# The end of a recommendation kernel in another order: what stands ahead of the head's results

## The chip, the cores and the metric

The kernel runs on one core of a Trainium2 chip. The metric is the device time of one execution in microseconds (us), lower is better; the time before is the median of three runs. The profile is of one execution, taken by the hardware profiler. Engines are named as the profile names them: PE (TensorE matmul) and PEld (its weight loads), DVE (VectorE), ACT (ScalarE), POOL (GpSimd), SP (SyncE, which here only starts DMAs). L142 is line 142 of the kernel.

## The reference

A batch of 16,384 users, each with a history of 200 items, an item and a category; embeddings have 64 numbers, the attention unit 36 hidden numbers.

```python
def dice(x, alpha, axis):
    mean = jnp.mean(x, axis=axis, keepdims=True)
    var = jnp.var(x, axis=axis, keepdims=True)
    p = jax.nn.sigmoid((x - mean) * jax.lax.rsqrt(var + EPS))
    return x * (p + alpha * (1.0 - p))
u = u_emb[user]          # 16384 x 64
it = i_emb[item]
c = c_emb[cate]
h = i_emb[hist]          # 200 x 16384 x 64
itb = jnp.broadcast_to(it[None], h.shape)
feat = jnp.concatenate([h, itb, h - itb, h * itb], axis=-1)
a = dice(feat @ au_W1 + au_b1, au_alpha, axis=1)
w = a @ au_W2 + au_b2
cur = jnp.sum(w * jax.lax.stop_gradient(h), axis=0)
z = jnp.concatenate([u, it, c, cur], axis=-1)
z = dice(z @ W1 + b1, alpha1, axis=0)
z = dice(z @ W2 + b2, alpha2, axis=0)
return z @ W3 + b3
```

Each history position has its own mean and variance over the whole batch, and so has each layer of the head. That is why a chunk of rows can't be finished in one go: the statistics over all eight chunks come first.

## The kernel before, in words

**Chunks and steps.** The batch is cut into ND = 8 chunks of 2,048 rows. A history position is eight steps, one for each chunk, so K = 200 x 8 = 1600 steps `step(k)`. In step k POOL gathers the embedding rows of chunk k (`fetch`, L118: one gather brings 128 rows, so 16 or 15 per step); some rows are brought instead by single DMAs on the queues of SP and ACT. One step later the chunk is transposed (`turn`, L137) and multiplied (`product`, L142); three steps later its hidden values `xs` are added up and measured (L387, L392); LAG = 10 steps later it is weighed:

- `gate(k)`: ACT writes the sigmoid of `xs` to `pg` (L362).
- `weights(k)`: DVE makes one weight per row from it (L366, L367, L368, L369, L372), which end up in `pg`.
- `weigh(k)`: DVE multiplies the history rows by their weights (L382, the last reader of `pg`) and adds the product to the running sum `cur[c]` (L384).

**The head's first layer**, one chunk at a time, is where the change is. `head_fetch(c)` has POOL gather the users' rows into `spare[c % 4]` (16 gathers, L118), and SP loads the transposed category rows `cT[c % 4]` and item rows `itT`. `head_known(c)` transposes the finished sum `cur[c]` into `hT` (DVE, L137, four instructions) and has PE multiply category, item and sum. `head_users(c)` transposes the users into `uT` (L137; for the last chunk in two parts, 12 columns of rows and then 4) and has PE multiply them. Both use `head_layer`, which writes two results in PSUM: `pz[1]` (32 rows, by the weights `w1b`) and `pz[0]` (128 rows, by `w1a`). A chunk's eight pairs of weights and data make 16 matmuls, each two instructions on PE. Then ACT adds the biases and writes `zb` (L616) and `za` (L619, into the `xs` buffer of the same chunk), and DVE takes their statistics (`measure_head`, L595; `zb` once per four chunks).

**What sets the order.** The code is written out by hand (`manual_schedule`): each engine gets its instructions in the order of the calls and works them off in that order; semaphores make it wait for data and for free buffers. The end, from L625 on, calls for j = 0 to 7 the loads of chunk j, then one or two steps, then `head_known` and `head_users` for the chunks whose sum is finished. After it come the statistics of the first layer over all chunks (`head_moments`), the second and third layer, and the output.

In the profile's names, `rows` are history or user rows, `itp` stands for `cT` and `uT` (they share storage), `px` for `pz[0]` and `pz[1]`, `xs` for `za`, and `rows` also for `zb`, which lies in a buffer of rows.

Of the kernel before, what the change touches and what calls it, by code (L numbers as in the profile page):

```python
# [10 lines left out]
AF = mybir.ActivationFunctionType  # L11
# [10 lines left out]
LAG = 10  # L22
XR = 8
TURNED = 2
ITEMS = 4
# [14 lines left out]
def din_kernel(  # L40
# [93 lines left out]
    def transpose(dst, of, n0=0, n1=TD):  # L134
        for i in range(2):
            for e in range(2):
                nc.vector.transpose(by_tile(dst[ts(e, D)], i)[:, n0:n1], of[ts(i, D), n0:n1, ts(e, S)])  # L137
# [222 lines left out]
    def gate(k, between):  # L360
        i = k // ND % 3
        nc.scalar.activation(pg, xs[k % XR], AF.Sigmoid, bias=shifts[i], scale=rstds[i])  # L362
        between()
# [34 lines left out]
    def load_items(k):  # L398
        nc.sync.dma_start(itT[k % ITEMS], items[k % ND])
# [31 lines left out]
    def step(k):  # L431

        def has(j):
            return 0 <= j < K

        def some(n):
            by_scalar.pump(min(by_scalar.done + n, by_scalar.until(k + 1)))

        if has(k + 2):
            load_items(k + 2)  # L440
        if has(k):
            l, c = divmod(k, ND)
            if c == 0 and l + 2 < L:
                load_hist_ids((l + 2) % IDX, l + 2)
            if c == 0 and l + 2 == L:
                load_ids(ids[1], r_user)
            if c == 1 and l + 2 < L:
                load_list(l + 2)
            fetch(k)
            q, m = side(k) or (None, None)  # L450
            taken = q and q.take(m)
        by_sync.pump(by_sync.until(k + 1))
        norm = has(k - 3) and (k - 3) % ND == ND - 1
        if has(k - LAG) and not norm:
            gate(k - LAG, lambda: some(5))
        if has(k):
            place(k, taken)
        if has(k - 1):
            turn(k - 1)
        if has(k - 3):  # L460
            hidden(k - 3)
            measure(k - 3)
        if norm:
            moments((k - 3) // ND)
            some(20)
            if has(k - LAG):
                gate(k - LAG, lambda: some(5))
        by_scalar.pump(by_scalar.until(k + 1))
        if has(k - 1):
            product(k - 1)  # L470
        if has(k - LAG):
            weights(k - LAG)
            weigh(k - LAG)
        if has(k) and k % ND == ND - 2 and k // ND + 2 < L:
            scale_list(k // ND + 2)
# [117 lines left out]
    def measure_head(i, j, t):  # L593
        for h in range(2):
            nc.vector.bn_stats(zst[i][:, 2 * j + h, :], t[:, ts(h, CH)])  # L595

    def head_fetch(c):
        for n in range(TD):
            i = c * TD + n
            gather(spare[c % 4], ids[1][:, i : i + 1], n, u_emb)  # L600
# [3 lines left out]
    def head_layer(pairs, first, last):  # L604
        layer(pz[1][:S], [(w1b[:, f], t) for f, t in pairs], first=first, last=last)
        layer(pz[0], [(w1a[:, f], t) for f, t in pairs], first=first, last=last)

    def head_known(c):
        transpose(hT[c % TURNED], cur[c].rearrange("p (n d) -> p n d", d=D))
        head_layer(((2, cT[c % 4]), (1, itT[(K + c) % ITEMS]), (3, hT[c % TURNED])), True, False)  # L610

    def head_users(c):
        for n0, n1 in ((0, LATE), (LATE, TD)) if c == ND - 1 else ((0, TD),):
            transpose(uT[c % 4], spare[c % 4], n0, n1)
        head_layer(((0, uT[c % 4]),), False, True)
        nc.scalar.activation(zb[c // 4][ts(c % 4, S)], pz[1][:S], AF.Identity, bias=b1b)  # L616
        if c % 4 == 3:
            measure_head(1, c // 4, zb[c // 4])
        nc.scalar.activation(za[c], pz[0], AF.Identity, bias=b1a)  # L619
        measure_head(0, c, za[c])  # L620

    with tc.manual_schedule():
        for k in range(K):
            step(k)
        k, c = K, 0  # L625
        for j in range(ND):
            head_fetch(j)
            nc.sync.dma_start(cT[j % 4], cates[j])
            load_items(K + j)
            while k <= K + (j + 1) * LAG // ND:  # L630
                step(k)
                k += 1
            while c <= j and k > K + LAG - ND + c:
                head_known(c)
                head_users(c)
                c += 1
        assert k > K + LAG - 1 and c == ND

        def head_moments(parts):

            n = len(parts)
            mv = small.tile([P, n, 2], F32, tag=f"hmv{n}", name="hmv")
            for j, (i, _) in enumerate(parts):
                nc.vector.bn_aggr(mv[:, j], zst[i].rearrange("p c s -> p (c s)"))
            for j, (_, same) in enumerate(parts):
                nc.tensor.matmul(pg[:, j : j + 1], same, mv[:, j, 0:1], start=True, stop=True)
            mean = small.tile([P, n], F32, tag=f"hmean{n}", name="hmean")
            nc.vector.tensor_copy(mean, pg[:, :n])
            dev = small.tile([P, n], F32, tag=f"hdev{n}", name="hdev")
            nc.vector.tensor_sub(dev, mv[:, :, 0], mean)  # L650
            nc.vector.tensor_mul(dev, dev, dev)
            nc.vector.tensor_add(dev, dev, mv[:, :, 1])
            for j, (_, same) in enumerate(parts):
                nc.tensor.matmul(py[:, j : j + 1], same, dev[:, j : j + 1], start=True, stop=True)
            rstd = small.tile([P, n], F32, tag=f"hrstd{n}", name="hrstd")
            root(rstd, py[:, :n])
            shift = small.tile([P, n], F32, tag=f"hshift{n}", name="hshift")
            nc.vector.scalar_tensor_tensor(shift, mean, -1.0, rstd, ALU.mult, ALU.mult)
            return [(rstd[:, j : j + 1], shift[:, j : j + 1]) for j in range(n)]

        temps = [hm, *flat_rows[6:8]]
        turns = iter(range(1000))

        def dice(dst, z, norm, al1, al):
            p = temps[next(turns) % len(temps)]
            nc.scalar.activation(p, z, AF.Sigmoid, bias=norm[1], scale=norm[0])
            nc.vector.tensor_scalar(p, p, al1, al, ALU.mult, ALU.add)
            nc.vector.tensor_mul(dst, p, z)

        z2 = flat_rows[8:]  # L670
        na, nb = head_moments([(0, same_a), (1, same_b)])
        ab = uT[:2]

        def second(c):
            nc.scalar.activation(z2[c], pz[c % 4], AF.Identity, bias=bias2)
            measure_head(2, c, z2[c])

        def first(c):
            dice(cur[c], za[c], na, al1a, ala)
            if c % 4 == 0:  # L680
                dice(ab[c // 4], zb[c // 4], nb, al1b, alb)

        first(0)
        for c in range(ND):
            if c + 1 < ND:
# [62 lines left out]
```

## Time and profile before

| | |
|---|---|
| median of three runs | 50,439.11 us |
| lowest and highest | 50,419.98 and 50,472.64 us |
| span of the profiled execution, first to last instruction | 31,394.9 us |
| median less span | 19,044.2 us |
| busy: POOL, DVE, PE | 23,583.2, 23,566.6 and 10,269.6 us |
| gathers from the item table on POOL | 24,828, of 944 ns each |
| the end: first transpose of a finished sum | at 31,117.71 us |
| last gather of users | at 31,233.05 us |
| last statistics of the head's first layer begin | at 31,320.92 us |

The profile gives no time of the profiled execution other than its span; what lies between the span and the runs' time is not seen in it. Times "at" count from the first instruction. In the profile's rows a group's idle time is that of its engine just before it, and the arrow names what ended the wait. The timeline has a start, a duration, the engine, the line, the operation with output and input, and in brackets the idle time before it.

### The profile page before, as it was taken

The numbers are of one execution on the slowest core, as the hardware profiler recorded it, in microseconds if no ns is written. First come the engines' busy times: TensorE is split into PE (matmuls) and PEld (weight loads), VectorE is DVE, ScalarE is ACT, GpSimd is POOL, SyncE is SP. The second block draws the span as 40 slices with busy tenths as digits, with TensorE's granted clock in tenths as the row PEclk, the third lists the DMA queues.
The fourth block names the chain that finished last, engine by engine and source line by source line (L and its number), as shares of the span: only waits on it lengthen the run. The fifth ranks groups of instructions, "written<-read, shape, count | busy, mean of one in ns | idle before, by whom it ended". The sixth has DMA issues, their size and how long they took to land.

```text
span 31394.9 us, 344371 instructions
## 1 busy us (share of the span) xinstructions
PE 10269.6 (33%) x13700; PEld 3833.8 (12%) x13700; DVE 23566.6 (75%) x35131; ACT 3842.2 (12%) x4167; POOL 23583.2 (75%) x24979
## 2 busy tenths in 40 slices
PE   5333333333333333333333333333333333333334
PEld 2111111111111111111111111111111111111111
DVE  6777777777777777777777777777777777777777
ACT  0111111111111111111111111111111111111111
POOL 7777777777777777777777777777777777777776
PEclk7666666666666666666666666666666666666666
DMA  2222222222222222222222222222222222222221
GB/s 60 56 56 56 55 56 55 56 56 56 56 55 56 56 55 56 55 56 56 55 56 56 56 56 55 56 56 55 56 55 56 56 56 55 56 56 55 56 56 47
DMA packets 1461708, 1742.53 MB, mean 56 GB/s; under 512 B 824822, under 2 KB 850678, under 8 KB 1459126
## 3 DMA queue, kind: packets, MB, share of 16 engines
q0 software_dynamic: 799104, 819.88, 14.8%
q1 hardware_dynamic: 544246, 885.58, 8.9%
q10 hardware_dynamic: 115776, 15.04, 0.3%
q14 instruction: 2475, 20.28, 0.2%
q8 instruction: 107, 1.75, 0.0%
HBM read 1709.80 MB, written 8.52 MB: 55 GB/s over the span
## 4 chain that ended last, share of the span: by engine, by line
POOL 62%; issue 23%; DMA 6%; DVE 6%; PE 1%; ACTq 1%; ACT 1%; SPq 0%; POOLq 0%; DVEq 0%
POOL rows L118 62%; DMA rows<-in_L_rec_i_emb,idx 6%; DVE hT L137 1%; PE py L525 1%; DVE py L366 1%; DVE pg L367 1%; DVE py L368 0%; DVE st L392 0%; DVE xs L387 0%; ACT pg L362 0%; ACTq L328 0%; PE px L142 0%; DVE other L413 0%; DVE t L158 0%; DVE t L157 0%
## 5 line engine op out<-in xcount | busy, mean ns | idle before, releaser
L118 POOL DMA_INDIRECT rows<-in_L_rec_i_emb,idx x24828 | 23446.7, 944 | 7606.2 <-issue 7362.7
L142 PE MATMUL px<-hT,blk_h 128*128 128x512 f32 x6400 | 5951.4, 1085 | 19937.4 <-DVE xs L387 19904.6
L137 DVE STREAM_TRANSPOSE hT<-rows 64x512 f32<-64x512 f32 x6400 | 4514.8, 705 | 6602.8 <-DMA rows<-in_L_rec_i_emb,idx 6298.5
L142 PEld LDWEIGHTS px<-hT,blk_h 128*128 128x128 f32 x6400 | 1873.7, 323 | 23103.2 <-DVE xs L387 21419.7
L142 PE MATMUL px<-hm,blk_m 128*128 128x512 f32 x6400 | 4114.5, 777 | 995.5 <-DVE hm L403 995.5
L362 ACT ACTIVATE pg<-xs,sh,rs 128x1024 f32<-128x1024 f32 x1600 | 1931.7, 1207 | 16036.0 <-issue 7328.8
L396 ACT COPY py<-hT 128x1024 f32<-128x1024 f32 x1600 | 1626.1, 1016 | 9705.2 <-DVE hT L137 9643.5
L142 PEld LDWEIGHTS px<-hm,blk_m 128*128 128x128 f32 x6400 | 1797.5, 285 | 3951.9 <-DVE hm L403 2034.6
L366 DVE SCALAR_TENSOR_TENSOR py<-pg,au_1al,xs 128x1024 f32<-128x1024 f32 x1600 | 2068.0, 1293 | 81.0 <-ACT pg L362 8.6
L392 DVE BATCH_NORM_STATS2 st<-xs 128x6 f32<-128x512 f32 x3200 | 2057.8, 685 | 54.9
L367 DVE STREAM_TRANSPOSE pg<-py 128x1024 f32<-128x1024 f32 x1600 | 2024.9, 1266 | 54.5
L368 DVE TENSOR_REDUCE py<-pg 128x32 f32<-128x1024 f32 x1600 | 1972.6, 1233 | 54.4
L382 DVE TENSOR_TENSOR py<-rows,pg 128x1024 f32<-128x1024 f32 x1592 | 1955.9, 1229 | 54.6
L387 DVE TENSOR_TENSOR xs<-px,itp 128x1024 f32<-128x1024 f32 x1600 | 1958.3, 1224 | 50.4
L403 DVE TENSOR_TENSOR hm<-py,itT 128x1024 f32<-128x1024 f32 x1600 | 1934.2, 1209 | 80.2 <-ACT py L396 79.9
L384 DVE TENSOR_TENSOR cur<-py,cur 128x1024 f32<-128x1024 f32 x1592 | 1948.6, 1224 | 55.0
L372 DVE SCALAR_TENSOR_TENSOR pg<-py,au_bias,part 32x16 f32<-32x16 f32 x6400 | 1530.2, 239 | 225.6
L369 DVE COPY part<-py 64x32 f32<-64x32 f32 x1600 | 310.6, 194 | 55.5
L358 ACT COPY rows<-act_rows 128x64 f32<-128x64 f32 x450 | 109.8, 244 | 721.9 <-issue 682.2
L358 ACT COPY rows<-sp_rows 128x64 f32<-128x64 f32 x450 | 109.9, 244 | 519.9 <-issue 403.2
L524 DVE TENSOR_SCALAR cur<-pg,rows 128x512 f32<-128x512 f32 x150 | 103.0, 743 | 92.8 <-PE pg L517 89.6
L525 PE MATMUL py<-cur,cur 128*128 128x512 f32 x300 | 156.1, 663 | 42.6 <-DVE cur L524 38.2
(159 smaller groups left out, 2075.5 us busy)
## 6 DMA issues: line engine op xcount, KB each, us to landing
sp_rows<-in_L_rec_i_emb SPq DMA_DIRECT2D x57600, 0.2 KB
act_rows<-in_L_rec_i_emb ACTq DMA_DIRECT2D x57600, 0.2 KB
itT<-items SPq DMA_DIRECT2D x1608, 512.0 KB
rows<-in_L_rec_i_emb,idx POOLq DMA_INDIRECT x24828
idx<-in_r_hist SPq DMA_DIRECT2D x200, 64.0 KB
lists<-in_r_hist SPq DMA_DIRECT2D x600, 1.0 KB
items<-itT SPq DMA_DIRECT2D x8, 512.0 KB
cates<-xs SPq DMA_DIRECT2D x8, 512.0 KB
```

The costliest lines, as they stand in the source:

```text
L118: nc.gpsimd.indirect_dma_start(out=dst[:, n, :], out_offset=None, in_=table, in_offset=bass.IndirectOffsetOnAxis(ap=ids, axis=0),)
L137: nc.vector.transpose(by_tile(dst[ts(e, D)], i)[:, n0:n1], of[ts(i, D), n0:n1, ts(e, S)])
L142: nc.tensor.matmul(dst[:, ts(i, CH)], lhsT, rhs[:, ts(i, CH)], start=(first and j == 0), stop=(last and j == len(pairs) - 1), skip_group_c ...
L362: nc.scalar.activation(pg, xs[k % XR], AF.Sigmoid, bias=shifts[i], scale=rstds[i])
L366: nc.vector.scalar_tensor_tensor(py, pg, au_1al, xs[k % XR], ALU.mult, ALU.mult)
L367: nc.vector.transpose(pg, py)
L368: nc.vector.reduce_sum(total, pg.rearrange("p (n a) -> p n a", a=S), axis=mybir.AxisListType.X)
L382: nc.vector.tensor_mul(of, rows[k % ROWS], w.unsqueeze(2).to_broadcast([P, TD, D]))
L384: nc.vector.tensor_add(cur[k % ND], py, cur[k % ND])
L387: nc.vector.tensor_add(xs[k % XR], px[k % 2], itp[k % ND])
L392: nc.vector.bn_stats(stats[l % 3][:, 2 * c + i, :], xs[k % XR][:, ts(i, CH)])
L403: nc.vector.tensor_mul(hm, py, itT[k % ITEMS])
```

## The change

The calls of the end are put in another order; nothing is added or left out. `head_known` now holds only the products with category and item, a new `head_sums` the transpose of the sum and its products, and a new `head_measure` the statistics. `head_load` bundles the three loads of a chunk and is called three chunks ahead of `head_sums`. For each chunk: weights and weighted sum, the sigmoid of the chunk after it, the loads, the statistics of the chunk before, the sum's products, the users' products and ACT's two results, and then the next chunk's products with category and item.

```diff
     def head_known(c):
+        head_layer(((2, cT[c % 4]), (1, itT[(K + c) % ITEMS])), True, False)
+
+    def head_sums(c):
         transpose(hT[c % TURNED], cur[c].rearrange("p (n d) -> p n d", d=D))
-        head_layer(((2, cT[c % 4]), (1, itT[(K + c) % ITEMS]), (3, hT[c % TURNED])), True, False)
+        head_layer(((3, hT[c % TURNED]),), False, False)
...
         nc.scalar.activation(zb[c // 4][ts(c % 4, S)], pz[1][:S], AF.Identity, bias=b1b)
+        nc.scalar.activation(za[c], pz[0], AF.Identity, bias=b1a)
+
+    def head_measure(c):
         if c % 4 == 3:
             measure_head(1, c // 4, zb[c // 4])
-        nc.scalar.activation(za[c], pz[0], AF.Identity, bias=b1a)
         measure_head(0, c, za[c])
...
-        k, c = K, 0
-        for j in range(ND):
-            head_fetch(j)
-            nc.sync.dma_start(cT[j % 4], cates[j])
-            load_items(K + j)
-            while k <= K + (j + 1) * LAG // ND:
-                step(k)
-                k += 1
-            while c <= j and k > K + LAG - ND + c:
-                head_known(c)
-                head_users(c)
-                c += 1
+        first_weighed = LAG - ND
+        for c in range(first_weighed + 1):
+            head_load(c)
+            step(K + c)
+        head_known(0)
+        for c in range(ND):
+            k = K - ND + c
+            if c:
+                weights(k)
+                weigh(k)
+            if c + 1 < ND:
+                gate(k + 1, lambda: None)
+            if c + first_weighed + 1 < ND:
+                head_load(c + first_weighed + 1)
+            if c:
+                head_measure(c - 1)
+            head_sums(c)
+            head_users(c)
+            if c + 1 < ND:
+                head_known(c + 1)
+        head_measure(ND - 1)
```

With the new lines, L616 and L619 become L619 and L620, and everything behind the end's loop moves down by 18 lines.

On DVE, around chunk 1 (`xs_88` and `xs_89` are `za` of chunks 0 and 1; `hT_87<-cur_117` the transposed sum of chunk 1, `itp_131<-rows_71` its users, and `xs_90` the hidden values of chunk 2, whose weights begin with L366):

```order
 L382 TENSOR_TENSOR py<-rows_79,pg 128x1024
 L384 TENSOR_TENSOR cur_117<-py,cur_117 128x1024
+L595 BN_STATS zst_3768<-xs_88 128x6 x2
 L137 STREAM_TRANSPOSE hT_87<-cur_117 64x512 x4
 L137 STREAM_TRANSPOSE itp_131<-rows_71 64x512 x4
-L595 BN_STATS zst_3768<-xs_89 128x6 x2
 L366 SCALAR_TENSOR_TENSOR py<-pg,au_1al,xs_90 128x1024
 L367 STREAM_TRANSPOSE pg<-py 128x1024
```

Chunk 1's statistics stood between its transposes and chunk 2's weights; now chunk 0's stand behind chunk 1's weighted sum, and chunk 2's weights follow the transposes at once.

On ACT, in the first chunks (`pg<-xs_89` is the sigmoid of chunk 1; `rows_74<-px_67` and `xs_88<-px_66` are the results `zb` and `za` of chunk 0):

```order
 L362 ACTIVATE pg<-xs_88,sh_146,rs_143 128x1024
-L616 ACTIVATE rows_74<-px_67,b1b 32x1024
-L619 ACTIVATE xs_88<-px_66,b1a 128x1024
 L362 ACTIVATE pg<-xs_89,sh_146,rs_143 128x1024
-L616 ACTIVATE rows_74<-px_67,b1b 32x1024
-L619 ACTIVATE xs_89<-px_66,b1a 128x1024
+L619 ACTIVATE rows_74<-px_67,b1b 32x1024
+L620 ACTIVATE xs_88<-px_66,b1a 128x1024
 L362 ACTIVATE pg<-xs_90,sh_146,rs_143 128x1024
```

The sigmoid of chunk 1 stood behind the two results of chunk 0 and now stands ahead of them; so in every later chunk.

On PE, the second half of chunk 1's products (`itp_127` category, `itT_97` item, `hT_87` sum, `itp_131` users; `px_67` by `w1b`, `px_66` by `w1a`):

```order
 L142 MATMUL px_66<-itp_127,w1a 128x512
 L142 MATMUL px_66<-itT_97,w1a 128x512
-L142 MATMUL px_66<-hT_87,w1a 128x512
 L142 MATMUL px_66<-itp_127,w1a 128x512
 L142 MATMUL px_66<-itT_97,w1a 128x512
-L142 MATMUL px_66<-hT_87,w1a 128x512
+L142 MATMUL px_67<-hT_87,w1b 32x512 x2
+L142 MATMUL px_66<-hT_87,w1a 128x512 x2
 L142 MATMUL px_67<-itp_131,w1b 32x512 x2
 L142 MATMUL px_66<-itp_131,w1a 128x512 x2
```

The sum's products stood among those with category and item and held them up until the sum was transposed; now all of the latter come first. The orders of POOL's gathers and of SP's loads are the same as before.

More of the change, by code (lines that the diff above doesn't have):

```diff
@@ L616, in head_users, with head_load @@
         nc.scalar.activation(zb[c // 4][ts(c % 4, S)], pz[1][:S], AF.Identity, bias=b1b)
+        nc.scalar.activation(za[c], pz[0], AF.Identity, bias=b1a)
+    def head_measure(c):
         if c % 4 == 3:
             measure_head(1, c // 4, zb[c // 4])
-        nc.scalar.activation(za[c], pz[0], AF.Identity, bias=b1a)
         measure_head(0, c, za[c])
+    def head_load(c):
+        head_fetch(c)
+        nc.sync.dma_start(cT[c % 4], cates[c])
+        load_items(K + c)
     with tc.manual_schedule():
@@ L624, in din_kernel @@
             step(k)
-        k, c = K, 0
-        for j in range(ND):
-            head_fetch(j)
-            nc.sync.dma_start(cT[j % 4], cates[j])
-            load_items(K + j)
-            while k <= K + (j + 1) * LAG // ND:
-                step(k)
-                k += 1
-            while c <= j and k > K + LAG - ND + c:
-                head_known(c)
-                head_users(c)
-                c += 1
-        assert k > K + LAG - 1 and c == ND
+        first_weighed = LAG - ND
[19 more added lines that the diff above has]
+        head_measure(ND - 1)
         def head_moments(parts):
```

## The prediction

> **What bounds the kernel now.** I read the page first, then the timeline of each engine over the last 400 us, the chain of waits there, and the busy time of the stages.
>
> ```profile
> span 31394.9 us, 344371 instructions
> PE 10269.6 (33%) x13700; PEld 3833.8 (12%) x13700; DVE 23566.6 (75%) x35131; ACT 3842.2 (12%) x4167; POOL 23583.2 (75%) x24979
> L118 POOL DMA_INDIRECT rows<-in_L_rec_i_emb,idx x24828 | 23446.7, 944 | 7606.2 <-issue 7362.7
> ```
>
> For over 31 ms the kernel is a line of gathers on POOL: one takes 0.944 us and the next begins some 0.30 us later, whatever the other engines do. The change touches none of that. It rewrites the end, where the gathers run out. The stages of the end (start and end, width, busy time of PE, PEld, DVE, ACT and POOL, granted TensorE clock, DMA share, GB/s):
>
> ```profile
> 31118.00:31234.00 116.00, 75.73 (x148) 21.98 (x148) 63.44 (x90) 13.38 (x12) 87.75 (x93) 0.82 0.25 63
> 31234.00:31322.00 88.00, 56.25 (x105) 15.53 (x104) 45.73 (x68) 12.17 (x11) 0.00 (x0) 0.79 0.00 1
> 31322.00:31395.00 73.00, 48.42 (x108) 17.57 (x108) 56.18 (x102) 29.97 (x26) 0.00 (x0) 0.81 0.01 2
> ```
>
> In the middle row POOL has nothing left, no DMA moves, and yet PE is busy for 56 of 88 us and DVE for 46: the two take turns. Those 88 us are what the change can reach. The last 73 us (the head's second half) keep their instructions.
>
> One chunk in that stage, first on DVE (start, duration, idle before it and what ended the idle), then on ACT, with the chain that ended last in between:
>
> ```profile
> 31278.27 2.88 DVE L137 STREAM_TRANSPOSE itp<-rows 64x512 f32<-64x512 f32 x4
> 31293.63 1.29 DVE L595 BATCH_NORM_STATS2 zst<-xs 128x6 f32<-128x512 f32 x2 [12.48 <-ACT xs L619]
> 31294.83 1.28 DVE L366 SCALAR_TENSOR_TENSOR py<-pg,au_1al,xs 128x1024 f32<-128x1024 f32 x1
> ...
> 31301.30 1.23 DVE L384 TENSOR_TENSOR cur<-py,cur 128x1024 f32<-128x1024 f32 x1
> 31302.63 2.88 DVE L137 STREAM_TRANSPOSE hT<-cur 64x512 f32<-64x512 f32 x4
> 31305.54 3.62 DVE L137 STREAM_TRANSPOSE itp<-rows 64x384 f32<-64x384 f32 x8
> 31318.99 1.29 DVE L595 BATCH_NORM_STATS2 zst<-rows 128x6 f32<-128x512 f32 x2 [9.83 <-ACT rows L616]
> 31320.92 1.29 DVE L595 BATCH_NORM_STATS2 zst<-xs 128x6 f32<-128x512 f32 x2 [0.64 <-ACT xs L619]
> ```
> ```profile
> 31304.10 15.64 PE px L142 x28
> 31319.77 1.12 ACT xs L619
> ```
> ```profile
> 31266.22 1.20 ACT L362 ACTIVATE pg<-xs,sh,rs 128x1024 f32<-128x1024 f32 x1
> ...
> 31293.49 1.20 ACT L362 ACTIVATE pg<-xs,sh,rs 128x1024 f32<-128x1024 f32 x1
> 31317.86 1.10 ACT L616 ACTIVATE rows<-px,b1b 32x1024 f32<-32x1024 f32 x1 [23.16 <-PE px L142]
> ```
>
> The two sigmoids (L362) stand 31293.49 - 31266.22 = 27.27 us apart: that is one chunk. It is a ring without overlap: sigmoid, weights and weighted sum on DVE (31294.83 to 31302.63, 7.80 us), half of the sum's transpose, 15.64 us of matmuls, 1.12 us of ACT, 1.20 us of statistics, and only then the next chunk's weights. DVE's wait of 12.48 us in every chunk, ended by L619, is the ring's mark:
>
> ```profile
> PE px L142 <- DVE hT L137: 82.6, 8, 17.4
> ...
> DVE zst L595 <- ACT xs L619: 73.3, 8, 12.5
> ```
>
> Over the eight chunks DVE waits 73.3 us for the results, and PE 82.6 us for the transposed sum.
>
> **The change part by part.** No instruction is added or removed; all keep their shapes. Four things move.
>
> *Statistics of the chunk before (L595) go behind the next chunk's weighted sum.* In DVE's row the wait for L619 then falls behind 7.80 us of work that needs no result of the head. The next sigmoid needs `pg` free (the weighting multiply, L382, is its last reader) and stands ahead of the results on ACT, so it ends long before DVE comes to it: DVE first transposes the sum (2.88 us) and the users (2.88 us). I cost both edits at nothing on the path. The cover is those 5.8 us for the sigmoid's 1.2, and the 7.8 us for the matmuls on the users and the two ACT results. If that cover went, DVE would wait for the rest.
>
> *DVE is then the steady user.* Per chunk: 7.80 + hT 2.91 (31302.63 to 31305.54) + users 2.88 + statistics 1.20 (31293.63 to 31294.83) = 14.8 us; 1.2 us more behind chunk 3, for the second group's statistics.
>
> *PE's matmuls with category and item go ahead of the sum.* Each matmul is two instructions, 32 per chunk. Their pace has two values:
>
> ```profile
> 31194.97 1.02 PE L142 MATMUL px<-itT,w1b 128*32 128x512 f32 x2
> 31198.06 1.05 PE L142 MATMUL px<-hT,w1b 128*32 128x512 f32 x2 [2.07 <-DVE hT L137]
> ...
> 31222.44 1.92 PE L142 MATMUL px<-hT,w1b 128*32 128x512 f32 x2 [9.82 <-DVE hT L137]
> 31224.14 1.91 PE L142 MATMUL px<-itp,w1b 128*32 128x512 f32 x2
> 31225.85 1.91 PE L142 MATMUL px<-itT,w1b 128*32 128x512 f32 x2
> 31227.56 1.29 PE L142 MATMUL px<-hT,w1b 128*32 128x512 f32 x2
> 31228.77 1.12 PE L142 MATMUL px<-itp,w1a 128*128 128x512 f32 x2
> ...
> 31317.75 1.98 PE L142 MATMUL px<-itp,w1a 128*128 128x512 f32 x4
> ```
> ```profile
> 31198.06 12.73 PE px L142 x28
> ```
>
> After 2.07 us of idle time PE goes on at full pace (28 instructions in 12.73 us, 0.45 each with the gaps); after 9.82 us it starts at half ((31227.56 - 31222.44) / 6 = 0.853 us each), for about 6 us. The same 28 cost 15.64 us in the last chunk. Thus before pays 2.9 us for a slow start in most chunks. Afterwards 32 x 0.45 = 14.4 us of PE work stand against 14.8 us of DVE work. PE gets 16 of the 32 (7.2 us) while DVE weighs (7.8 us), so its gaps are around a microsecond and it stays at pace. [...]
>
> *Loads (users' gathers, cT, itT) are asked for three chunks ahead.* POOL's row keeps its order, so what matters is whether a slot is late. It was not:
>
> ```profile
> 31075.99 2.86 DVE L137 STREAM_TRANSPOSE hT<-rows 64x512 f32<-64x512 f32 x4 [5.70 <-DMA rows<-in_L_rec_i_emb,idx]
> ```
> ```profile
> 31073.24 0.94 POOL L118 DMA_INDIRECT rows<-in_L_rec_i_emb,idx  x1 [0.30 <-issue]
> 31074.48 0.95 POOL L118 DMA_INDIRECT rows<-in_L_rec_u_emb,idx  x1 [0.30 <-issue]
> ...
> 31233.05 0.94 POOL L118 DMA_INDIRECT rows<-in_L_rec_u_emb,idx  x1 [0.30 <-issue]
> ```
>
> The 128 gathers of users start from 31074.48 to 31233.05, (31233.05 - 31074.48) / 127 = 1.249 us apart: 20.0 us per chunk without a stop. This becomes the new limit, since a chunk needs only 14.8 us. A gather's data can be used 31075.99 - 31073.24 = 2.75 us after its start (the last history gather and the transpose that waits for it). SP's queue is passed by two loads per chunk; each waits for a slot that was read two chunks earlier, and nothing else stands behind it.
>
> The sum, in the profiled execution's time. Chunk 0's transposes stand where they stood:
>
> ```profile
> 31117.71 2.88 DVE L137 STREAM_TRANSPOSE hT<-cur 64x512 f32<-64x512 f32 x4
> ```
>
> - Chunk c begins its users' transpose at 31120.6 + 14.8 c, with 1.2 more from c = 4: chunk 5 at 31195.8. Its users are usable at 31074.48 + 95 x 1.249 + 2.75 = 31195.9: a tie.
> - Chunk 6 would begin at 31210.6; its users come at 31074.48 + 111 x 1.249 + 2.75 = 31215.9. From here POOL leads. That transpose ends at 31218.8.
> - Chunk 7: 7.80 + 1.20 + 2.91 gives 31230.7. Its users come in two parts: twelve of sixteen columns (their transpose is about 2.2 of the 3.62 us), then the last four, usable at 31233.05 + 2.75 = 31235.8. So 31235.8 + 1.4 = 31237.2.
> - The last 8 matmul instructions begin at about half of that transpose: 31236.5 + 8 x 0.45 = 31240.1. L619's successor 1.12: 31241.2. Statistics 1.29: 31242.5.
>
> Before, the last statistics end at 31320.92 + 1.29 = 31322.2. The gain is 79.7 us; I take 79, because every step has a few hundredths of a microsecond of issue. Span 31,394.9 - 79 = 31,316 us. The profile states only the span. The runs' median is 50,439.1 us, so 19,044 us lie outside of the span; I hold them constant and carry the gain over: 50,439.1 - 79 = 50,360 us, 0.16% less. The runs shown stand from 50,419.98 to 50,472.64, so about 0.2% (101 us) is what a measurement can tell from no change. The forecast is a real gain that lies just under that line.
>
> **Unknowns and their bounds.** The mid-case of the clock: if PE started slowly in every chunk, a chunk would cost 14.4 + 2.9 = 17.3 us of PE, which then leads DVE. From 31119.2 (first half of chunk 0's transpose) 10.1 us for its last 16 instructions and 7 x 17.3 give 31250.4, 10.3 us later than above: a gain of 69. On the other side nothing goes below the gathers' end, 31235.8. What stands behind it, the transpose, matmuls, ACT and statistics, cannot be hidden, so 80 is the ceiling inside the span.
>
> **The rivals.**
>
> 1. *The 19,044 us are not a constant, but time in which everything is slower than in the profile.* Then the gain scales by 50,439.1 / 31,394.9 = 1.607: 127 us, 50,312. Nothing in the page speaks for it; the steady 944 ns of 24,828 gathers speak for a chip that runs evenly.
> 2. *The gathers alone are slower in the timed runs.* 19,044 over the 24,979 POOL instructions is 0.76 us each. A chunk of gathers would cost 16 x (1.249 + 0.76) = 32.1 us, more than the 27.27 us ring, which would then be hidden already in the kernel before: no change, 50,439. That is also the case in which the change does not do what it says. The profile can't exclude it, but shows gathers that end 88 us ahead of the ring.
> 3. *PE never reaches its full pace, and the change is slower.* Each chunk's 32 instructions then cost 32 x 0.853 + about 1 us of gaps = 28.3 us in one row on PE, more than the ring of 27.27. From 31119.2, 16 x 0.853 + 7 x 28.3 end at 31331, and with 1.12 and 1.29 us at 31333.4: 11 us later than before, 50,450. It decides once PE's 32 instructions exceed 26 us, that is 0.82 us each. Against it: 0.45 us in the row of 28 above, after a short gap; and the new order has fewer gaps.
>
> **How the numbers follow.** Forecast (69 to 80 us of gain): 0.74. Rival 1: 0.07. Rival 2: 0.10. Rival 3: 0.02. The remaining 0.07 is for medians that move by more than the runs shown, to both sides alike. The forecast's own range: 50,360 with the runs' spread (-19 and +34 around their median) is 50,340 to 50,404. The range for 8 in 10 takes in the ends of rivals 1 and 2: 50,305 to 50,440. Faster by over 0.2% means under 50,338: rival 1, a fifth of the forecast by the runs' spread, and a little of the rest, 0.24. Slower by over 0.2% needs 50,540: no mechanism here reaches it, so 0.03 from the rest. Within: 0.73.
>
> **What would show it.** In the profile after: no wait of DVE for L620 (the former L619) of more than a microsecond; L362 ahead of L619 and L620 on ACT; PE instructions 0.43 us apart through the end stage, and no start at 0.85 after chunk 1; DVE waiting for the users' gathers in chunks 6 and 7; the last user gather still at about 31233; the last L595 of `za` near 31243. The prediction is wrong if the users' gathers start later than now, if PE waits for cT or itT, or if the time outside the span moves.

## The result, and the profile after

The changed kernel takes 50,371.1 us (median of 20 runs, 50,343.0 to 50,408.4), the kernel before 50,438.4 us (20 runs, 50,420.0 to 50,472.6). The ratio is 0.9985, interval 0.9979 to 0.9992: 67 us less, where 79 were forecast. That lies inside the forecast's range and under the 0.2% named there, and the interval does not reach 1. How it came about differs from the forecast in two places, and the runs below are about these.

The page of the changed kernel: span, POOL's and DVE's share, the chain by engine, and the history's gathers.

```profile
span 50359.7 us, 344371 instructions
PE 11205.4 (22%) x13700; PEld 3875.5 (8%) x13700; DVE 23541.9 (47%) x35131; ACT 3756.0 (7%) x4167; POOL 23591.3 (47%) x24979
...
SPq 42%; issue 37%; ACTq 16%; DVE 3%; ACT 1%; PE 1%; another core or an unknown queue 0%; DMA 0%; POOL 0%; DVEq 0%; POOLq 0%
...
L118 POOL DMA_INDIRECT rows<-in_L_rec_i_emb,idx x24828 | 23454.9, 945 | 26505.3 <-DVE py L382 18667.6
```

The span is now the whole time (50,359.7 of 50,361.4 us), with the same number of instructions. So the 19 ms that stood outside the span in the first profile of before stand inside it here. POOL's gathers take 945 ns each, as before; POOL now waits 18,668 us for DVE's weighing (L382). What is slow is shown by SP's row loads of the main loop (two groups of 36 in the changed kernel, start and duration):

```profile
31070.86 38.97 SPq L328 DMA_DIRECT2D sp_rows<-in_L_rec_i_emb  x36
...
31110.38 13.77 SPq L328 DMA_DIRECT2D sp_rows<-in_L_rec_i_emb  x36
```

The same 36 instructions take 39.0 us or 13.8 us. POOL gathers until 31,093.6, beside much of the first group, and pauses beside most of the second:

```profile
31119.86 0.94 POOL L118 DMA_INDIRECT rows<-in_L_rec_i_emb,idx  x1 [26.25 <-DVE py L382]
```

The slow pace ends on SP, ACT and DVE alike at 31,099.6, 6.9 us after the last gather began (31,092.67). In the slow stretches many short instructions of SP, ACT and DVE start 0.70 or 1.40 us apart (DVE's L159, L157 and L158 at 31,094.04, 31,095.44 and 31,096.84). Long ones (1.2 us and up) hardly show it (L382's 1,592, of 1.23 us each, stood idle 57.0 us in all, 0.04 each), and not every short one does. Two of DVE's small operations in the changed kernel, four in each step (L372) and a longer row of them behind each layer (L157; behind the second bar the idle time):

```profile
L372 DVE SCALAR_TENSOR_TENSOR pg<-py,au_bias,part 32x16 f32<-32x16 f32 x6400 | 1526.9, 239 | 231.9 <-issue 5.2
L157 DVE TENSOR_TENSOR t<-rs 128x1 f32<-128x1 f32 x800 | 129.2, 161 | 931.3 <-DVE rs L159 565.4
```

That is 0.04 us of idle time an instruction against 1.16. In the first profile of before L157 had 27.7 us in all.

The end of the changed kernel by stage, in the columns of the prediction's first table: the head's first layer, a part of it, and the second half of the head.

```profile
50124.00:50286.00 162.00, 119.81 (x240) 34.40 (x240) 109.64 (x159) 25.18 (x23) 60.36 (x64) 0.86 0.12 33
50250.00:50286.00 36.00, 34.12 (x75) 9.83 (x73) 29.58 (x47) 7.75 (x7) 0.00 (x0) 1.00 0.00 0
50286.00:50360.00 74.00, 48.88 (x108) 17.68 (x108) 56.58 (x102) 29.97 (x26) 0.00 (x0) 0.80 0.01 2
```

In the middle row PE works 34 of 36 us at full clock and DVE 30: the turn-taking of before is gone. The first row holds more than that. ScalarE there (L362 sigmoid, L619 and L620 the results; in brackets the idle time before and what ended it):

```profile
50137.65 1.20 ACT L362 ACTIVATE pg<-xs,sh,rs 128x1024 f32<-128x1024 f32 x1
50161.17 1.10 ACT L619 ACTIVATE rows<-px,b1b 32x1024 f32<-32x1024 f32 x1 [22.32 <-remote]
50172.43 1.11 ACT L620 ACTIVATE xs<-px,b1a 128x1024 f32<-128x1024 f32 x1 [10.15 <-remote]
...
50222.24 1.10 ACT L619 ACTIVATE rows<-px,b1b 32x1024 f32<-32x1024 f32 x1 [32.19 <-remote]
50225.83 1.11 ACT L620 ACTIVATE xs<-px,b1a 128x1024 f32<-128x1024 f32 x1 [2.49 <-remote]
...
50252.89 1.10 ACT L619 ACTIVATE rows<-px,b1b 32x1024 f32<-32x1024 f32 x1 [10.49 <-PE px L142]
50254.86 1.11 ACT L620 ACTIVATE xs<-px,b1a 128x1024 f32<-128x1024 f32 x1 [0.87 <-PE px L142]
```

The sigmoid stands ahead of the results, as forecast. But ScalarE waits 22 and 32 us for the first results of chunks 1 and 3, where 10.5 is usual, and no recorded work ends that wait. At the second results these chunks are 21 and 23 us late. None of the four waits for a gather: in the trace the semaphores that they wait for, 128 and 127, are raised by PE and ScalarE alone. PE's last products for chunk 1 are recorded here:

```profile
50147.41 1.91 PE L142 MATMUL px<-itp,w1b 128*32 128x512 f32 x4
50149.24 1.98 PE L142 MATMUL px<-itp,w1a 128*128 128x512 f32 x4
```

They end by 50,151.2, and ACT gets the first of the two results at 50,161.17 and the second at 50,172.43. The two are 11.26 us apart, for 4 matmuls and 4 weight loads: 1.41 us an instruction, the pace of the slow stretches (1.97 us apart at 50,252.89, 3.59 in chunk 3). PE's rows, whose ends the profile models, don't show this: by them PE was done 10 us before the first of the two came. POOL at that time:

```profile
50130.94 0.94 POOL L118 DMA_INDIRECT rows<-in_L_rec_u_emb,idx  x1 [60.07 <-DVE itp L137]
...
50169.63 0.94 POOL L118 DMA_INDIRECT rows<-in_L_rec_u_emb,idx  x1 [0.30 <-issue]
50180.82 0.94 POOL L118 DMA_INDIRECT rows<-in_L_rec_u_emb,idx  x1 [10.25 <-DVE itp L137]
...
50219.51 0.94 POOL L118 DMA_INDIRECT rows<-in_L_rec_u_emb,idx  x1 [0.30 <-issue]
```

These are two bursts of 32 gathers. Chunk 1's first result comes inside the first burst, its second 2.8 us after the start of that burst's last gather, and chunk 3's first 2.7 us after that of the second (50,222.24). Whether the gathers hold the results up is the question of most runs. The same stage on DVE, changed kernel (hT is the transposition of a chunk's sum):

```profile
50124.88 2.88 DVE L137 STREAM_TRANSPOSE hT<-cur 64x512 f32<-64x512 f32 x4
...
50173.57 1.29 DVE L595 BATCH_NORM_STATS2 zst<-xs 128x6 f32<-128x512 f32 x2 [20.54 <-ACT xs L620]
...
50223.37 1.29 DVE L595 BATCH_NORM_STATS2 zst<-rows 128x6 f32<-128x512 f32 x2 [19.67 <-ACT rows L619]
...
50257.43 2.86 DVE L137 STREAM_TRANSPOSE hT<-cur 64x512 f32<-64x512 f32 x4
...
50272.06 2.86 DVE L137 STREAM_TRANSPOSE hT<-cur 64x512 f32<-64x512 f32 x4
...
50285.31 1.29 DVE L595 BATCH_NORM_STATS2 zst<-xs 128x6 f32<-128x512 f32 x2 [0.64 <-ACT xs L620]
```

Undisturbed chunks stand 14.63 us apart. In what follows "the first layer" is the time from the first hT to the end of the last L595: here 50,286.6 - 50,124.9 = 161.7 us.

### The profile page after: what moved, and what is told of

The parts are those of the page before. It is cut to its first block, busy times and chain, and to the rows that moved or that the text cites. A ratio compares the mean times of both kernels' runs of the same rounds, so it can differ in the third digit from the quotient of the medians.

```text
span 50359.7 us, 344371 instructions
## 1 busy us (share of the span) xinstructions
PE 11205.4 (22%) x13700; PEld 3875.5 (8%) x13700; DVE 23541.9 (47%) x35131; ACT 3756.0 (7%) x4167; POOL 23591.3 (47%) x24979
## 4 chain that ended last, share of the span: by engine, by line
SPq 42%; issue 37%; ACTq 16%; DVE 3%; ACT 1%; PE 1%; another core or an unknown queue 0%; DMA 0%; POOL 0%; DVEq 0%; POOLq 0%
SPq L328 35%; ACTq L328 14%; SPq L321 5%; ACTq L321 1%; SPq L399 1%; DVE py L366 1%; DVE hm L403 1%; SPq L289 1%; ACT py L396 0%; DVE pg L367 0%; DVE hT L137 0%; PE py L525 0%; DVE py L368 0%; ACT pg L362 0%
## 5 line engine op out<-in xcount | busy, mean ns | idle before, releaser
L142 PE MATMUL px<-hm,blk_m 128*128 128x512 f32 x6400 | 4915.1, 912 | 24582.9 <-DVE hm L403 24472.1
L362 ACT ACTIVATE pg<-xs,sh,rs 128x1024 f32<-128x1024 f32 x1600 | 1931.8, 1207 | 33014.7 <-issue 23975.5
L366 DVE SCALAR_TENSOR_TENSOR py<-pg,au_1al,xs 128x1024 f32<-128x1024 f32 x1600 | 2068.8, 1293 | 1112.0 <-ACT pg L362 1059.4
L382 DVE TENSOR_TENSOR py<-rows,pg 128x1024 f32<-128x1024 f32 x1592 | 1956.6, 1229 | 57.0 <-issue 2.1
L372 DVE SCALAR_TENSOR_TENSOR pg<-py,au_bias,part 32x16 f32<-32x16 f32 x6400 | 1526.9, 239 | 231.9 <-issue 5.2
L157 DVE TENSOR_TENSOR t<-rs 128x1 f32<-128x1 f32 x800 | 129.2, 161 | 931.3 <-DVE rs L159 565.4
L158 DVE SCALAR_TENSOR_TENSOR t<-t,v 128x1 f32<-128x1 f32 x808 | 130.7, 162 | 885.2 <-DVE t L157 719.1
L159 DVE SCALAR_TENSOR_TENSOR rs<-t,rs 128x1 f32<-128x1 f32 x800 | 128.3, 160 | 813.2 <-DVE t L158 678.2
```

Source lines behind the costliest of these rows:

```text
L142: nc.tensor.matmul(dst[:, ts(i, CH)], lhsT, rhs[:, ts(i, CH)], start=(first and j == 0), stop=(last and j == len(pairs) - 1), skip_group_c ...
L366: nc.vector.scalar_tensor_tensor(py, pg, au_1al, xs[k % XR], ALU.mult, ALU.mult)
L382: nc.vector.tensor_mul(of, rows[k % ROWS], w.unsqueeze(2).to_broadcast([P, TD, D]))
```

## The experiments

**e1: the kernel before, profiled once more.**

> The kernel before, unchanged, profiled once more beside the changed one. The changed kernel's profile has a span of 50,359.7 us, nearly its whole time, while the profile of before has 31,394.9: so the 19,044 us that I held constant outside of the span lie inside it in the timed runs. Theory 1 (stretches in which SP and ACT issue their single-row DMAs slowly, L328): time 50,420 to 50,473 as before, span within 3 us of it, 36 DMAs of SP's L328 in 14 to 46 us instead of 14, gathers still 0.944 us each; the end from the first transpose of a finished sum to the last statistics of the first layer takes 204 us as in the first profile, plus at most a few stretches of 30 us. Theory 2 (everything slower by 1.607): the same end takes 329 us, and one gather 1.5 us.

Measured: 50,419.8 us, and a span of 50,418.0. Its DVE:

```profile
50121.50 2.88 DVE L137 STREAM_TRANSPOSE hT<-cur 64x512 f32<-64x512 f32 x4
...
50235.35 1.29 DVE L595 BATCH_NORM_STATS2 zst<-rows 128x6 f32<-128x512 f32 x2 [27.25 <-ACT rows L616]
...
50289.81 1.28 DVE L595 BATCH_NORM_STATS2 zst<-xs 128x6 f32<-128x512 f32 x2 [12.06 <-ACT xs L619]
...
50344.08 1.29 DVE L595 BATCH_NORM_STATS2 zst<-xs 128x6 f32<-128x512 f32 x2 [0.64 <-ACT xs L619]
```

First layer 223.9 us against 204.5 in the first profile of before: the ring with its 12 us waits, and one late result (27.25 us). Like with like, the change takes 223.9 - 161.7 = 62.2 us off this stage. That is the timed gain within its interval, and the first profile was of another condition than the timed runs.

**e2 and e3: no row loads by SP and ACT, in before and after.** The edit in both:

```diff
-BY_SP = ((0, 0), (0, 3), ..., (3, 3))
-BY_ACT = ((0, 1), (0, 4), ..., (3, 4))
+BY_SP = ()
+BY_ACT = ()
```

> Kernel before with BY_SP and BY_ACT empty: no single-row DMAs on SP and ACT; POOL gathers the sixteenth row block itself. 25,872 gathers instead of 24,972. Theory 1 (the row DMAs are what is slow in the timed runs): 25,872 x 1.249 = 32,314 us plus some 280 us of end: 32,500 to 32,800 us, ratio to before 0.645 to 0.65. Theory 2 (everything is slower) or gathers alone slower (2.01 us each): 52,000 us, ratio 1.03.

> The changed kernel with BY_SP and BY_ACT empty. Theory 1: a clean end, 69 to 80 us less than e2 (79 by the sum of the prediction), its end from the first transpose of a finished sum to the last statistics 125 us against 204 in e2, PE at 0.43 us per instruction throughout, DVE waiting for the users' gathers in chunks 6 and 7. Rival (the changed kernel's own profile: 163 us for the same end, with ACT waiting 10 to 32 us ahead of its results): 163 us and about 40 us less than e2.

Measured: e2 38,329.2 us (38,327.0 to 38,338.9; ratio to before 0.7599, interval 0.7587 to 0.7612), e3 38,265.7 us (38,257.1 to 38,273.9; 0.7586, interval 0.7573 to 0.7598). I expected e2 at 32,500 to 32,800; it is slowed too, only less. For e3 I expected a clean first layer of 125 us; it took 160.4, near the rival's 163. The change is worth 63.5 us here, in the first layer 222.5 - 160.4 = 62.1. This pair is steadier than the first, so the next runs build on it. And e3 is the version that beats both kernels, by 24%.

**e4: the users' rows of chunks 4 to 7 not gathered** (on e3).

```diff
-        for n in range(TD):
+        for n in range(TD if c < 4 else 0):
```

> The changed kernel with all row loads of the main loop on POOL (as e3_after_pool), and the users' rows of chunks 4 to 7 not gathered: the 64 gathers are left out, so these chunks work on what lies in the slots. Against e3 (38,265.7 us, first layer of the head 160.4 us from the first transposition of a sum to the last statistics). Theory S1, TensorE's results are told late to ScalarE while POOL issues gathers: the two stalls at chunks 1 and 3 (transposition to transposition 35.8 and 38.4 us in e3 against 14.7 elsewhere, 44.8 us too much together) vanish, all chunks stand 14.6 to 15 us apart, the first layer takes 114 to 121 us, the time is 38,221 us (38,205 to 38,235). Rival S2, the stalls are TensorE's own (its burst of two chunks' products, its clock): both stay, first layer 158 to 162 us, time 38,266 us (38,250 to 38,280). Rival S3, the gathers themselves were the limit by their order on POOL (chunk waits for its users): only the wait before the users' transposition would go, at most a few us.

Measured: first layer 117.0 us, time 38,194.8 us (38,192.8 to 38,215.0). The chain and the stages there:

```profile
38026.62 113.07 PE px L142 x240
```
```profile
38025.00:38069.00 44.00, 42.38 (x87) 12.07 (x88) 42.48 (x61) 10.04 (x10) 0.00 (x0) 0.92 0.14 48
38069.00:38142.00 73.00, 70.68 (x154) 20.72 (x152) 66.53 (x99) 14.60 (x13) 0.00 (x0) 1.00 0.04 15
```

No late result is left, and the chain is one piece of PE from end to end, 113.07 / 240 = 0.471 us an instruction. Both stalls belong to the late gathers: S1 holds, S2 and S3 fall. Part of the time's 71 us below e3 is the chip (the kernel before took 50,390 there, 50,439 with e3, which makes 37 us at this length).

**e9 and e11: what about the gathers does it.** Each replaces these 64 gathers, e9 by clearing the slot on POOL, e11 by plain transfers of as many rows on SP's queue:

```diff
+            if c < 4:
                 gather(spare[c % 4], ids[1][:, i : i + 1], n, u_emb)
+            else:
+                nc.gpsimd.memset(flat_rows[c % 4], 0.0)                      # e9
+                nc.sync.dma_start(spare[c % 4][:, n, :], u_emb[ts(i, P)])    # e11
```

> e4 with POOL kept busy without transfers: in place of each of the 64 gathers of the users' rows of chunks 4 to 7 (left out, these chunks work on zeros) POOL clears a whole slot (128x1024). Theory S1 in its narrow form (it is the gathers, their descriptors or their transfers): no stall, first layer 114 to 121 us as in e4. Rival, any busy stretch of POOL keeps TensorE's results from being told: stalls of 15 us or more come back as in e3, first layer above 140 us. A third way, DVE slowed by POOL's work on the same memory: DVE's transpositions and statistics above 0.72 and 0.69 us each, chunks longer but without one long gap.

> e3 with the 64 gathers of the users' rows of chunks 4 to 7 replaced by 64 plain transfers on SP's queue of the same size and shape (128 rows of 64 values, 32 KB, into the same slots at the same place of the program; 128 consecutive rows instead of the gathered ones, so these chunks work on other users). POOL is idle there, as many rows are moved as in e3. [...] If it is the transfer of many short rows, or what is recorded of it: stalls of 15 us or more, first layer 140 to 165 us as in e3. [...]

Measured: first layer 117.0 us in both (38,193.4 and 38,204.6 us, one run each). POOL's group in e9, then PE's piece of the chain in e9 and in e11:

```profile
L603 POOL MEMSET rows<- 128x1024 f32 x64 | 60.8, 952 | 61.4 <-DVE itp L137 57.9
```
```profile
38004.98 113.06 PE px L142 x240
```
```profile
38016.26 113.02 PE px L142 x240
```

POOL as busy as with gathers (952 ns against 945) does no harm, and as many short rows moved by another queue do none (SP issues them in four groups of 16, each within 8 us, so faster than POOL). What is left is the gather as POOL does it. Whether a plain transfer issued by POOL would do the same, no run tried.

**e10: the order of before, without those gathers.** The same edit as e4, on e2.

> e2 (the order before the change, all row loads on POOL) with the users' rows of chunks 4 to 7 not gathered, as e4 for the changed order; these chunks work on what lies in the slots. If the stalls go here too, the ring of gate, weights, weighing, sum and results alone is left: chunks 26 to 27 us apart but one of 18 to 19 us, first layer 200 to 207 us against 222.5 in e2. With e4's 117.0 the change would be worth 83 to 90 us without stalls, and 62 with them. If the stalls aren't of the gathers' making in this order: 218 to 225 us.

Measured: first layer 207.1 us (38,288.8 us, one run). The waits in it (total, times, longest) and two sums' transpositions:

```profile
DVE zst L595 <- ACT xs L619: 75.8, 8, 12.5
```
```profile
38167.37 2.88 DVE L137 STREAM_TRANSPOSE hT<-cur 64x512 f32<-64x512 f32 x4
38194.68 2.88 DVE L137 STREAM_TRANSPOSE hT<-cur 64x512 f32<-64x512 f32 x4
```

A ring of 27.31 us, as the prediction read it. Without stalls the change is worth 207.1 - 117.0 = 90.1 us. The late gathers cost the old order 222.5 - 207.1 = 15.4 us and the new one 160.4 - 117.0 = 43.4, so 28.0 of the 90.1 are lost again: 62.1.

**e5 and e6: each part alone** (on e3). e5 keeps the sigmoid ahead and the late statistics, with all products of item, category and sum in one group again:

```diff
-        head_layer(((3, hT[c % TURNED]),), False, False)
+        head_layer(((2, cT[c % 4]), (1, itT[(K + c) % ITEMS]), (3, hT[c % TURNED])), True, False)
...
-            if c + 1 < ND:
-                head_known(c + 1)
```

e6 keeps the early products, with sigmoid and statistics where they were before:

```diff
+                gate(k, lambda: None)
                 weights(k)
...
-            if c + 1 < ND:
-                gate(k + 1, lambda: None)
...
-            if c:
-                head_measure(c - 1)
             head_sums(c)
             head_users(c)
+            head_measure(c)
```

> All row loads on POOL (compare e2 38,329.2 us without the change, e3 38,265.7 us with all of it). Only one part of the change: sigmoid of the next chunk ahead of the head's results, the statistics one chunk later; the products of item, category and sum stay together in one group behind the sum's transposition, then the users'. My theory, the ring gate-weights-sum-results was what set the pitch, and the gate's move ahead opens it: undisturbed pitch 15 to 17 us a chunk, first layer 160 to 175 us, time 38,266 to 38,280 us, so at least 50 of the 63 us. Rival, the products ahead of the sum are what counts: pitch 19 to 22 us, time 38,295 to 38,315 us.

> All row loads on POOL. Only the other part: products with item and category (and the result's sum over them) issued a chunk early, the sum's and the users' behind; the sigmoid of a chunk stays right before its weights and the statistics right behind the results, as before the change. My theory: the ring stays closed but loses the 4 product pairs of item and category, about 4.8 us of 26.4: undisturbed pitch 20 to 23 us, first layer 185 to 205 us, time 38,290 to 38,315 us, 15 to 40 of the 63 us. Rival, the split alone is enough: pitch below 17 us, time 38,265 to 38,280 us. Rival, it does nothing without the open ring: pitch 26 us, 38,329 us.

Measured: e5 38,257.1 us (38,253.9 to 38,258.6), e6 38,256.6 us (38,252.4 to 38,286.0), both 0.7591 of before, interval 0.7578 to 0.7603. First layers 179.7 and 181.6 us. Two undisturbed sums of e5, then of e6:

```profile
38149.45 2.86 DVE L137 STREAM_TRANSPOSE hT<-cur 64x512 f32<-64x512 f32 x4
38167.77 2.87 DVE L137 STREAM_TRANSPOSE hT<-cur 64x512 f32<-64x512 f32 x4
```
```profile
38156.98 2.88 DVE L137 STREAM_TRANSPOSE hT<-cur 64x512 f32<-64x512 f32 x4
38177.87 2.88 DVE L137 STREAM_TRANSPOSE hT<-cur 64x512 f32<-64x512 f32 x4
```

Pitches of 18.3 and 20.9 us against 27.3 and 14.63. For e5 I expected 15 to 17, a miss: a shorter ring is left. A sum's transposition stands behind the statistics of the chunk before. These wait for the results of the chunk before, and 28 of the 32 matmul instructions for them stand behind that chunk's own transposition. DVE's wait for the second result (L617 here) in an undisturbed chunk of e5:

```profile
38148.25 1.29 DVE L595 BATCH_NORM_STATS2 zst<-xs 128x6 f32<-128x512 f32 x2 [3.60 <-ACT xs L617]
```

e6's pitch is as expected, its time below the range expected. Yet e6 gains as much as e5, since in its slower pace only one result fell into a burst (one wait of 38.5 us on ACT, two in e5). So both parts are needed for 14.6, and the stalls blur what each is worth. In time the two can't be told from each other, nor, by these intervals, from e2 or e3.

**e8 and e3 again: eight slots for the users' rows,** so that the late gathers follow the early ones at once.

```diff
-    zb = flat_rows[4:6]
+    zb = [flat_rows[8], flat_rows[12]]
...
-            gather(spare[c % 4], ids[1][:, i : i + 1], n, u_emb)
+            gather(spare[c], ids[1][:, i : i + 1], n, u_emb)
...
-            transpose(uT[c % 4], spare[c % 4], n0, n1)
+            transpose(uT[c % 4], spare[c], n0, n1)
```

> e3 with eight slots for the users' rows instead of four (each chunk its own, the first results of layer b moved to two other slots), so that the gathers of chunks 4 to 7 no longer wait for chunks 0 to 3: they follow the first four at once and end about 28 us behind the first transposition of a sum, instead of 95. Theory S1 (results of TensorE are told late while POOL issues gathers): one stall until about 31 us behind that transposition, then every chunk 14.6 us; first layer 125 to 140 us against 160.4, and unless the steps ahead lose what the head gains (they now run beside gathers where POOL had waited 60 us), the time is 20 to 35 us below e3. Rival, the stalls are tied to chunks 1 and 3 whatever POOL does: first layer 155 to 165 us, time as e3. Rival, the stall only moves ahead of the first transposition: first layer below 125 us, but time within 15 us of e3.

> The kernel of e3 once more, for the comparison with e8 on the same chip: ratio to the kernel before 0.7586 as then (0.757 to 0.760), first layer 158 to 163 us with two stalls of 20 to 24 us.

Measured: e8 38,253.1 us (38,249.4 to 38,260.6), e3 again 38,241.9 us (38,236.1 to 38,264.9); ratios 0.7586 (0.7576 to 0.7596) and 0.7583 (0.7573 to 0.7593). The first layer of e8 takes 115.9 us, all chunks clean, 42.7 less than the 158.6 of e3 again, and the time is none the less the same. ScalarE's waits for L427 in the 190 us ahead of the head (total, times, longest), in e8 and in e3 again:

```profile
ACT pg L362 <- DVE sh L427: 59.2, 1, 59.2
```
```profile
ACT pg L362 <- DVE sh L427: 48.6, 2, 30.3
```

It is above all the wait for the last layer's moments on DVE, a row of tiny instructions (L409 to L427), which takes 38.0 us in e8 and 5.7 in e3 again. One and the same of them (L159) in e8, where it falls into the gathers and just behind them, and in e3 again, where POOL pauses:

```profile
38037.66 0.16 DVE L159 SCALAR_TENSOR_TENSOR rs<-t,rs 128x1 f32<-128x1 f32 x1 [1.24 <-DVE t L158]
```
```profile
38019.99 0.16 DVE L159 SCALAR_TENSOR_TENSOR rs<-t,rs 128x1 f32<-128x1 f32 x1
```

1.40 us from start to start instead of 0.20. The third way that was on record came true: the stall moved ahead, to another engine, and the first sum's transposition starts 27.7 us later in e8 (38,059.24 against 38,031.50). In e3 again chunk 3's first result comes at 38,119.14, 9 us before that burst's last gather starts: the results come out slowly during a burst, and it is not its end that lets them go.

**e7: 36 idle copies more on ScalarE in each step** (on e3), 57,708 in the 1,603 steps.

```diff
-        by_scalar.pump(by_scalar.until(k + 1))
+        for _ in range(36):
+            nc.scalar.copy(idle_to, idle_of)
```

> e3 with 36 copies of one column (128x1) more on ScalarE in each step of the main loop, 57,600 instructions in all, that nobody waits for; ScalarE is busy 9% of the span there. Against e3 38,265.7 us, in which POOL's gathers at 1.249 us start to start would need about 32,600 us. Theory R, what the run takes above its undisturbed pace goes by the number of instructions of all engines (19,044 us for 344,371 instructions in the kernel before, 55 ns each; about 5,700 us for 106,898 in e3, 53 ns each): 57,600 x 54 ns = 3.1 ms more, 41.4 ms (40.8 to 42.0). Rival, the cost is that of row transfers issued by SP and ACT alone, or of POOL's gathers: the time stays at 38,266 us (38,200 to 38,500).

Measured: 41,202.6 us (41,181.4 to 41,240.4), ratio 0.8176 (0.8163 to 0.8190). Against e3's ratio that is 0.0590 x 50,390 = 2,973 us, 51.5 ns a copy, near theory R's 54. It agrees with e2: 344,371 - 106,898 = 237,473 instructions fewer and 12,109 us less, 51.0 ns each. But the page of e7 shows where it goes, and that is no flat charge by count:

```profile
ACT idle_to L472 50%; DVE hT L137 5%; ACT py L399 3%; ACT pg L362 3%; DVE py L366 2%; DVE pg L367 2%; DVE py L368 2%; DVE py L382 2%; DVE hm L406 2%; DVE pg L372 2%; DVE xs L387 1%; DVE t L157 1%; DVE st L395 1%; DVE t L158 1%
...
L472 ACT COPY idle_to<-idle_of 128x1 f32<-128x1 f32 x57708 | 11026.7, 191 | 22036.6 <-ACT idle_to L472 15158.0
```

The copies are half of the chain. Each takes 191 ns and stands 382 ns idle ahead of it: most start 0.22 us apart, about a fifth 1.40 us. An engine that nobody waited for became the bound, because its short instructions were slowed. Theory R met the number and not the mechanism: it had nobody wait for the copies. Why two such different edits come to the same price an instruction stays open.

## Why the prediction was right or wrong

- **The time outside the span, held constant:** wrong. It lies inside the timed span (e1), in stretches of 0.70 or 1.40 us an instruction. By the prediction's own sign (the time outside the span moves) its account fails here. The carried-over gain was close because the main loop costs nearly the same in both kernels: the first sum's transposition starts at 50,121.5 us in e1 and at 50,124.9 in the changed kernel.
- **The ring of 27.27 us, opened by the sigmoid and the late statistics:** right. 27.31 us in e10. Of DVE's waits for the results, those of chunks 1 and 3 are left, and 4.81 us in the last chunk, where DVE has nothing else to do. The early products were needed too: e5 stops at 18.3 us.
- **DVE as the steady user, 14.8 us a chunk:** right in size, 14.63 measured. The chain names PE (e4), whose work and DVE's are about equal there.
- **PE at 0.45 us an instruction:** right where nothing stalls: a clean chunk's 32 take 14.67 us (50,240.02 to 50,254.69), at full granted clock from the second stretch of e4 on. In the changed kernel's trace PE started at 0.9 us an instruction behind 7.34 us of idle time in chunk 0 (50,126.36) and again behind the stalls (after 11.10 us at 50,162.33, 5.88 at 50,173.59 and 20.98 at 50,223.39), and in the clean chunks, the last one among them, it did not. In e5, behind a gap of 2.07 us, PE once went on at a granted clock of 1.00 (38,169 to 38,171; its next 28 instructions took 12.73 us) and once started at 0.50 (38,151 to 38,153; 14.43 us), so a gap that short is not always safe.
- **The users' gathers as the limit in chunks 6 and 7:** the step that failed. In the profile of the changed kernel, which is one of the timed runs, the gathers of the first four chunks were done 54 us ahead of the first sum's transposition, and no users' transposition waited for a row. Without that limit the prediction's sum ends at about 31,225.4 + 3.6 + 2.9 + 1.12 + 1.29 = 31,234 (3.6 for the last users' transposition, 2.9 for what is left of the matmuls behind it), a gain of 88 us; e10 and e4 show 90.1. In its place came a cost that the prediction had at nothing: gathers running beside the new, denser order hold up PE's results, 28.0 us more than in the old order. Two errors partly cancelled: the limit that wasn't there took some 10 us off the forecast gain, and the missing cost left 28 us in it. That 79 came as near as it did to 62 us by the traces and 67 timed is in part luck.
- **The ceiling of 80 us:** wrong for the same reason; 90.1 is there once the gathers are away.
- **The rivals:** none came whole. Rival 1's premise did, since the 19 ms are slow time inside the span, but it is short instructions that are slow, and the gain did not scale (127 us; 62 by the traces). A gather still takes 945 ns. PE keeps its full pace in the clean chunks (0.46 us an instruction).
- **What would show it:** L362 ahead of the results, right; no wait for L620 over 1 us, wrong in chunks 1 and 3 (20.54 and 2.31 us); no slow start of PE after chunk 1, wrong behind both stalls; DVE waiting for the users in chunks 6 and 7, wrong; the last statistics near the forecast place, wrong by the stalls.

## What to carry to other kernels

Check that the profile you reason from has the length of the timed runs; where the span is 62% of the time, profile another execution before you lay the rest aside as a constant. The gathers on POOL were not free for the others here, though POOL and the DMA engines had room (POOL busy for 60.4 of 162 us, the DMA share 0.12): beside such gathers, put long instructions, and keep rows of tiny ones and dense matmuls out of their bursts. In e8 moving such a burst only moved the cost, so count it in the stage that receives it.

## What the runs showed of the hardware

Beside indirect gathers, rows of short instructions on the other engines started 0.70 or 1.40 us apart: DVE's 128x1 arithmetic 1.40 instead of 0.20 us (e8 against e3 again), SP's 36 row loads in 39.0 instead of 13.8 us, and two results of PE 11.26 instead of 1.97 us apart. Not every short instruction was slowed: the fours of L372 stood idle 0.04 us each in the changed kernel and 0.57 in e3 (3,637.6 us for 6,400). Nor were long ones always spared: L382's, of 1.23 us, stood idle 0.04 us each in the changed kernel and 0.50 in e3 (789.4 us for 1,592). Neither POOL's clears of the same length nor plain transfers of as many rows by SP did anything of the kind (first layer 117.0 us in e9 and e11, 160.4 in e3). In e8 the slow pace outlasted the burst: DVE was still at 1.40 us when the last gather had begun 17 us before, behind 160 us without a pause. In the changed kernel's head, behind bursts of 40 us, the last late results came 2.8 and 6.3 us after the start of the last gather.

The first profile of before has the same gathers (944 ns each) and none of this (L157's 800 stood idle 27.7 us in all, against 931.3 in the changed kernel). The time of that execution is not on record, but no timed run of the kernel took less than 50,378 us. What differs there, through which part of the chip the gathers act, and whether PE works late or only reports late, stays open.
